# Expert blocks: tokens and weights fetched by SyncE with row numbers in registers, TensorE in a fixed order

## Chip, core and metric

The kernel runs on one core of one Trainium2 chip. The metric is the device time in microseconds. The kernel before took 1066.96 us, the median of three runs (1065.83 to 1073.68).

PE is TensorE (PEld its weight loads), DVE VectorE, ACT ScalarE, POOL GpSimd, SP SyncE. SP computes nothing here; it issues DMAs.

## The reference

One transformer block over 64 sequences of 32 tokens with 256 features (2048 tokens): cross-attention to 257 context rows, self-attention, and a feed-forward layer of 8 experts, of which each token uses the two (`K`) that score highest; an expert has `H` = 512 hidden features. All of it is f32. The change is in the last part:

```python
scores_BSN = jnp.einsum('bsd,nd->bsn', x, Wr) + br
w_BSN = jax.nn.softmax(scores_BSN, axis=-1)
_, idx_BSK = jax.lax.top_k(scores_BSN + biases_N[None, None, :], K)     
val_BSK = jnp.take_along_axis(w_BSN, idx_BSK, axis=-1)
val_BSK = val_BSK / jnp.sum(val_BSK, axis=-1, keepdims=True)
...
h_NM2H = jnp.einsum('md,ndh->nmh', x_MD, Wl1) + bl1[:, None, :]
a_NMH, b_NMH = (h_NM2H[..., :H], h_NM2H[..., H:])
y_NMD = jnp.einsum('nmh,nhd->nmd', jax.nn.silu(a_NMH) * b_NMH, Wl2) + bl2[:, None, :]
ew_MN = ew_MN.at[jnp.arange(M)[:, None], idx_MK].set(val_MK)
y_MD = jnp.einsum('mn,nmd->md', ew_MN, y_NMD)
```

and before it `x = x + xattn(layernorm(x), ctx)`, `x = x + attn(layernorm(x))`; the result is `x + ffn(layernorm(x))`.

## The kernel before

**Start-up.** The attention weights are multiplied into `w_qk` and `w_vo`, and the last context row's contribution is stored in memory as `u_last` (lines 126 to 164). The pool `raw` of these inputs is closed, and later pools take its room.

**Attention.** There are 16 tiles of 128 tokens (four sequences). The main loop (lines 590 to 621) goes through the 64 sequences; each step scores the next sequence (`cross_probs`), transposes the probabilities of this one and mixes its context (`probs_transposed`, `cross_mix`). Two generators run beside it, some steps at a time: `ahead` (the queries of the next two tiles) and `behind`, that is `rest(t)`: cross-attention's output, self-attention and `route(t)` of the tile that was just finished. `load_context` (line 316) fetches the context of the next tile into one of two buffers, and the rows of `u_last` into one of three.

**Routing.** `route` (line 506) normalises the tile into `xr` (256 features, 8 expert weights, the token's number: 265 words), ranks each token within its two experts through a running count `seen`, and scatters `xr` to two rows of `routed` in memory with two indirect DMAs of POOL (line 560). `routed` has 2048 rows for each of the 8 experts. The tile's `x`, with the second bias added, is stored to `out` by SP (line 574). After all tiles `seen` says how many tokens each expert has.

**Experts.** The counts are turned into 39 blocks of up to 128 tokens of one expert each (lines 643 to 688), on DVE, with every row number as a column of 128 words: `sources` (the row of `routed` that each token slot reads; slots beyond the count read one row of zeros, `NOROW`) and `wrows` (the rows of the weight matrix `wall`, with a number out of bounds where the buffer, used three blocks earlier, holds the same expert already). For each block, `gathered` reads 128 rows of `routed` and `weights` reads 128 rows of 12,320 bytes of `wall` (first weights, second weights and first biases of an expert) into one of three buffers `wbuf`; both are indirect DMAs of POOL (lines 704 and 693), and a row out of bounds is skipped. `prepared` transposes the tokens on PE, copies them with ACT (`bxT`), and finds `gate` and the target rows `to` on DVE. `hidden` is 16 products (32 PE instructions, since each f32 product is two) into `pa` and `pb`, four SiLU on ACT (`sa`) and four combinations on DVE (`g`). `combined` is four products of 256 columns (eight instructions) into `py`, a scaling by the gate on DVE (`y`), and an indirect DMA of POOL (line 764) that adds the 128 rows into `out`. Slots beyond the count add into spare rows behind the result.

**What sets the order.** The framework orders each engine's instructions by its own priorities and time estimates, and puts in the waits; no engine's order is written out. The loop at line 778 names block b's work so: gather and weights of b+2, `prepared` and `hidden` of b+1, `combined` of b. POOL's queue has gathers, weights and scatter-adds in one line, and each scatter-add into `out` waits for the one before.

Of the kernel before, what the change touches and what calls it, by code (L numbers as in the profile page):

```python
# [9 lines left out]
FP = mybir.dt.float32  # L10
# [6 lines left out]
P = 128  # L17
D = 256
# [11 lines left out]
NE = 8  # L30
HID = 512
CAP = TOK
NOROW = NE * CAP
RW = D + NE + 1
NBK = (2 * TOK) // P + NE - 1
WLEN = 2 * 2 * HID + 4 * D + 8
WBUF = 3
EPS = 1e-5
BASE = 10000.0
# [7 lines left out]
def block_kernel(  # L47
# [16 lines left out]
    wr_t: bass.AP,  # L64
    br: bass.AP,
    bias_n: bass.AP,
    wall: bass.AP,
    b2: bass.AP,
    out: bass.AP,
):  # L70
    nc = tc.nc

    const = ctx.enter_context(tc.tile_pool(name="const", bufs=1))
    ps = ctx.enter_context(tc.tile_pool(name="ps", bufs=3, space=PSUM))

# [23 lines left out]
    def load(dst, src):  # L99
        nc.sync.dma_start(out=dst, in_=src)  # L100
# [4 lines left out]
    w_qk = const.tile([P, XH, 2, KVD], FP, name="w_qk")  # L105
    w_vo = const.tile([P, XH, D], FP, name="w_vo")

    setup = ExitStack()
    raw = setup.enter_context(tc.tile_pool(name="raw", bufs=1))
    xwq_sb = raw.tile([P, XH // 2, D], FP, name="xwq_sb")  # L110
# [166 lines left out]

    seen = const.tile([P, NE], FP, name="seen")
    nc.gpsimd.memset(seen, 0.0)
    none = const.tile([P, D], FP, name="none")  # L280
    nc.gpsimd.memset(none, 0.0)
    load(routed[NOROW : NOROW + 1, 0:D], none[0:1, :].bitcast(U32))
    load(routed[NOROW : NOROW + 1, D:RW], none[0:1, 0 : RW - D].bitcast(U32))

    load(out[TOK : TOK + P, :], none)

    with ExitStack() as attn:
        kvp = attn.enter_context(tc.tile_pool(name="kv", bufs=2))
# [27 lines left out]
        def load_context(t):  # L316
            kvT = kvp.tile([P, 4, M], FP, tag="kvT", name=f"kvT{t}")
            kvA = kvp.tile([P, 4, MC, KVD], FP, tag="kvA", name=f"kvA{t}")
            ut = u_ring[t % 3]
            load(kvT, ctx_t[:, 4 * t : 4 * t + 4, :])  # L320
            load(kvA, ctx_a[:, 4 * t : 4 * t + 4, :, :])
            for h4 in range(4):
                load(ut[h4 * 32 : h4 * 32 + 16, :], u_last[h4, 16 * t : 16 * t + 16, :])
            return kvT, kvA, ut

        queries = {}

# [178 lines left out]
        def route(t):  # L506
# [52 lines left out]
            for k in range(2):  # L559
                nc.gpsimd.indirect_dma_start(  # L560
                    out=routed[:, :],
                    out_offset=bass.IndirectOffsetOnAxis(ap=slots[:, k : k + 1], axis=0),
                    in_=xr.bitcast(U32),
                    in_offset=None,
                )
            pw = ps.tile([NE, P], FP, tag="t", name=f"pw{t}")
# [19 lines left out]
        kvs = {0: load_context(0)}  # L586
        for _ in cross_queries(0):
            pass
        seqs = [(t, b) for t in range(NT) for b in range(4)]
# [2 lines left out]
        for n, (t, b) in enumerate(seqs):  # L592
            if b == 0:
                cT = wk.tile([P, XH, 4, SEQ], FP, tag="cT", name=f"cT{t}")
                lastT = wk.tile([P, 4, SEQ], FP, tag="lastT", name=f"lastT{t}")
                if t + 1 < NT:
                    kvs[t + 1] = load_context(t + 1)
                if t % 2 == 0 and t + 2 < NT:
                    for j in (t + 2, t + 3):
                        load(xs[j], x[j * P : (j + 1) * P, :])  # L600
                if t % 2 == 1 and t + 1 < NT:
                    ahead = cross_queries((t + 1) // 2)
            if b == 3:
# [12 lines left out]
            next(behind, None)  # L616
            next(ahead, None)
            if b == 3:
                for _ in behind:
                    pass  # L620
                behind = rest(t, cT, lastT, kvs[t][2])
        for _ in behind:
            pass


    with ExitStack() as ffn:
        tb = ffn.enter_context(tc.tile_pool(name="tb", bufs=1))
        xp = ffn.enter_context(tc.tile_pool(name="xp", bufs=3))
# [41 lines left out]
        source = small([NBK], "source")  # L670
        nc.vector.scalar_tensor_tensor(source, ebf, float(CAP), place, ALU.mult, ALU.add)
        nc.vector.scalar_tensor_tensor(
            source, source, float(-NOROW), valid, ALU.add, ALU.mult
        )
        sources = small([NBK], "sources", U32)
        nc.vector.tensor_scalar(sources, source, float(NOROW), None, ALU.add)
# [3 lines left out]
        wrow = small([NBK], "wrow")  # L680
        nc.vector.tensor_scalar(wrow, ebf, float(P), row, ALU.mult, ALU.add)
        held = small([NBK - WBUF], "held")
        nc.vector.tensor_tensor(held, ebf[:, WBUF:], ebf[:, :-WBUF], ALU.is_equal)
# [3 lines left out]
        wrows = small([NBK], "wrows", U32)  # L687
        nc.vector.tensor_copy(wrows, wrow)

        wbuf = [tb.tile([P, WLEN], FP, name=f"wbuf{i}") for i in range(WBUF)]  # L690

        def weights(b):
            nc.gpsimd.indirect_dma_start(  # L693
                out=wbuf[b % WBUF],
                out_offset=None,
                in_=wall[:, :],
                in_offset=bass.IndirectOffsetOnAxis(ap=wrows[:, b : b + 1], axis=0),
                bounds_check=NE * P - 1,
                oob_is_err=False,
            )  # L700

        def gathered(b):
            xg = xp.tile([P, RW], FP, tag="xg", name=f"xg{b}")
            nc.gpsimd.indirect_dma_start(  # L704
                out=xg.bitcast(U32),
                out_offset=None,
                in_=routed[:, :],
                in_offset=bass.IndirectOffsetOnAxis(ap=sources[:, b : b + 1], axis=0),
            )
            return xg  # L710

# [15 lines left out]
        W2, B1 = 4 * HID, 4 * HID + 4 * D  # L727

        def hidden(b, xT):
            w = wbuf[b % WBUF]  # L730
# [21 lines left out]
            return g  # L752

        def combined(b, g, gate, to):
            w = wbuf[b % WBUF]
            py = ps.tile([P, D], FP, tag="a", bufs=2, name=f"py{b}")
            for j in range(4):
                nc.tensor.matmul(  # L758
                    py, g[:, j, :], w[:, W2 + j * D : W2 + (j + 1) * D],
                    start=(j == 0), stop=(j == 3),  # L760
                )
            y = gp.tile([P, D], FP, tag="y", name=f"y{b}")
            nc.vector.tensor_scalar(y, py, gate, None, ALU.mult)  # L763
            nc.gpsimd.indirect_dma_start(  # L764
                out=out[:, :],
                out_offset=bass.IndirectOffsetOnAxis(ap=to[:, 0:1], axis=0),
                in_=y,
                in_offset=None,
                compute_op=ALU.add,
            )  # L770

        xgs = {0: gathered(0)}
        weights(0)
        xgs[1] = gathered(1)
        weights(1)
        ready = {0: prepared(0, xgs.pop(0))}
        gs = {0: hidden(0, ready[0][0])}
        for b in range(NBK):
            if b + 2 < NBK:
                xgs[b + 2] = gathered(b + 2)  # L780
                weights(b + 2)
            if b + 1 < NBK:
                ready[b + 1] = prepared(b + 1, xgs.pop(b + 1))
                gs[b + 1] = hidden(b + 1, ready[b + 1][0])
            _, gate, to = ready.pop(b)
            combined(b, gs.pop(b), gate, to)


# [51 lines left out]
```

## Time and profile before

| | |
|---|---|
| median of 3 runs | 1066.96 us |
| the profiled execution's own time | 1068.11 us |
| its span, first to last instruction | 1066.2 us |
| PE / PEld busy | 933.2 (88%) / 710.0 (67%) |
| DVE / ACT / POOL busy | 586.9 (55%) / 304.2 (29%) / 234.1 (22%) |
| granted PE clock, mean | 0.957 |
| POOL's DMA queue (q0) | 14640 packets, 52.61 MB |
| SP's DMA queue (q1) | 18500 packets, 28.15 MB |
| weight fetch (line 693), from issue to landing, median | 7.1 us |
| gather (line 704) | 4.1 us |
| scatter-add (line 764) | 5.3 us, from 3.7 to 7.8 |
| route scatter (line 560) | 2.7 us, from 2.5 to 5.6 |

Times in the profile count from the first instruction. The cross-attention starts at 51.37 us, the first route scatter is issued at 122.88, the last matmul on `seen` (line 644) runs at 783.66, the first gather is issued at 791.32, the first `pa` starts at 799.81, the first scatter-add at 813.01 and the last at 1059.62. A wait is read as "who waited, then whom for"; the idle time in brackets is that of the engine just before the instruction.

### The profile page before, as it was taken

The page shows a single profiled execution, that of the slowest core. Times are in us where ns is not written, and L with a number is a line of the kernel's source. Part 1 is how long each engine was busy: PE and PEld are TensorE (multiplying, and loading weights), DVE is VectorE, ACT ScalarE, POOL GpSimd, SP SyncE. Part 2 cuts the span into 40 slices and gives each one's busy share as a digit, 9 for nine tenths or more (in the row PEclk, how much of TensorE's full clock was granted, in tenths as well). Part 3 has the DMA queues.
Part 4 walks back from the last instruction along what each step waited for, and adds up shares of the span by engine and source line. Part 5 has one row for each costly group of instructions (what it writes and reads, how often), then busy time and mean ns, then how long its engine had stood idle before and what let it go on. Part 6 is the DMA issues. An engine that isn't in the chain of part 4 may idle for free. (4 is left out here: it accounts for less than half of the span.)

```text
span 1066.2 us, 14917 instructions
## 1 busy us (share of the span) xinstructions
PE 933.2 (88%) x5272; PEld 710.0 (67%) x5272; DVE 586.9 (55%) x2216; ACT 304.2 (29%) x999; POOL 234.1 (22%) x287
## 2 busy tenths in 40 slices
PE   6799989999997998999899899997628988999895
PEld 5567757766774775676577577664418877887785
DVE  3376685765768577566756857666232233332332
ACT  3352332322333232233323323222002222222221
POOL 3100111011011101101101110111033555555562
PEclk9999999998999999899999999998759999999998
DMA  8410101011010110101101010000025666667732
GB/s 259 136 40 4 55 23 38 26 34 54 23 38 26 33 50 28 38 21 38 55 4 55 23 38 26 31 16 13 3 94 206 197 221 178 218 218 219 218 42 25
DMA packets 33215, 81.72 MB, mean 77 GB/s; under 512 B 7435, under 2 KB 23316, under 8 KB 30068
## 3 DMA queue, kind: packets, MB, share of 16 engines
q0 software_dynamic: 14640, 52.61, 16.2%
q1 hardware_dynamic: 18500, 28.15, 8.5%
q8 instruction: 42, 0.69, 0.3%
q14 instruction: 33, 0.27, 0.1%
HBM read 91.66 MB, written 12.73 MB: 98 GB/s over the span
## 5 line engine op out<-in xcount | busy, mean ns | idle before, releaser
L366 ACT ACTIVATE pr<-s,nmx 128x257 f32<-128x257 f32 x256 | 119.8, 473 | 143.2 <-DVE nmx L365 142.4
L361 PE MATMUL s<-kvT,q 128*128 128x257 f32 x512 | 146.8, 413 | 6.8 <-ACT pr L366 6.6
L342 PE MATMUL pq<-xqT,w_qk 128*128 128x256 f32 x512 | 126.0, 388 | 6.2 <-ACT q L83 5.8
L399 PE MATMUL pa<-pt,kvA 128*128 128x512 f32 x256 | 125.6, 613 | 0.3
L361 PEld LDWEIGHTS s<-kvT,q 128*128 128x128 f32 x512 | 94.9, 200 | 39.1 <-ACT pr L366 16.3
L748 DVE SCALAR_TENSOR_TENSOR g<-pb,wbuf,sa 128x128 f32<-128x128 f32 x156 | 43.9, 344 | 127.5 <-PE pb L737 114.9
L409 PE MATMUL po<-w_vo,cT 128*128 128x256 f32 x512 | 113.3, 379 | 0.8 <-DVE cT L402 0.8
L365 DVE TENSOR_REDUCE nmx<-s 128x1 f32<-128x257 f32 x256 | 103.6, 418 | 13.9 <-PE s L361 12.8
L342 PEld LDWEIGHTS pq<-xqT,w_qk 128*128 128x128 f32 x512 | 93.3, 192 | 22.7 <-ACT q L83 8.1
L409 PEld LDWEIGHTS po<-w_vo,cT 128*128 128x128 f32 x512 | 97.0, 191 | 15.5 <-DVE cT L402 2.7
L758 PE MATMUL py<-wbuf,g 128*128 128x256 f32 x312 | 83.5, 392 | 13.2 <-DVE y L763 13.0
L737 PE MATMUL pa<-bxT,wbuf 128*128 128x128 f32 x624 | 80.7, 284 | 15.0 <-DMA wbuf<-in_wall,wrows 14.5
L737 PEld LDWEIGHTS pa<-bxT,wbuf 128*128 128x128 f32 x624 | 77.0, 198 | 23.3 <-issue 21.6
L303 POOL TENSOR_TENSOR rstdr<-ver,minus_half 128x1 f32<-128x1 f32 x16 | 9.3, 584 | 334.6 <-DVE ver L301 334.6
L737 PE MATMUL pb<-bxT,wbuf 128*128 128x128 f32 x624 | 76.4, 276 | 0.0
L391 ACT COPY pt<-tp 128x512 f32<-128x512 f32 x64 | 37.5, 585 | 135.3 <-PE tp L384 135.3
L744 ACT ACTIVATE sa<-pa,wbuf 128x128 f32<-128x128 f32 x156 | 44.5, 368 | 108.7 <-PE pa L737 108.7
L384 PE MATMUL tp<-ident,pr 128*128 128x128 f32 x512 | 74.3, 280 | 0.2
L372 DVE TENSOR_SCALAR pr<-pr,inv 128x256 f32<-128x256 f32 x256 | 73.9, 348 | 0.9
L737 PEld LDWEIGHTS pb<-bxT,wbuf 128*128 128x128 f32 x624 | 73.3, 193 | 0.0
L764 POOL DMA_INDIRECT out_x<-y,to x39 | 62.9, 1613 | 42.7 <-DVE gates L720 24.3
L399 PEld LDWEIGHTS pa<-pt,kvA 128*128 128x128 f32 x256 | 45.3, 193 | 40.1 <-issue 23.4
(194 smaller groups left out, 1194.8 us busy)
## 6 DMA issues: line engine op xcount, KB each, us to landing
kvT<-in_ctx_t SPq DMA_DIRECT2D x16, 514.0 KB, 3.3
kvA<-in_ctx_a SPq DMA_DIRECT2D x16, 512.0 KB, 3.6
x<-in_x SPq DMA_DIRECT2D x16, 128.0 KB, 3.0
out_x<-x SPq DMA_DIRECT2D x16, 128.0 KB, 1.7
xwq_sb<-in_xwq_t SPq DMA_DIRECT2D x1, 1024.0 KB
xwo_sb<-in_xwo SPq DMA_DIRECT2D x1, 1024.0 KB, 9.3
u_last<-u_sb SPq DMA_DIRECT2D x4, 256.0 KB, 3.8
u<-u_last SPq DMA_DIRECT2D x64, 16.0 KB, 1.7
```

The source lines that it names most:

```text
L342: nc.tensor.matmul(pq, w_qk[:, h, k, :], xqT[:, k, :], start=(k == 0), stop=(k == 1))
L361: nc.tensor.matmul(s, qb[:, g * P : (g + 1) * P], kvT[:, b, :], start=True, stop=True)
L365: nc.vector.tensor_reduce(nmx, s, AX.X, ALU.max, negate=True)
L366: nc.scalar.activation(pr[:, g, :], s, AF.Exp, bias=nmx, accum_out=sums[:, g : g + 1])
L372: nc.vector.tensor_scalar(pr[:, g, :ML], pr[:, g, :ML], inv[:, g : g + 1], None, ALU.mult)
L384: nc.tensor.transpose(tp[:, g * P : (g + 1) * P], pr[:, g, j * P : (j + 1) * P], ident)
L399: nc.tensor.matmul(pa, kvA[:, b, j, :], pts[j], start=(j == 0), stop=(j == MC - 1))
L409: nc.tensor.matmul(po, cT[:, h, :, :].rearrange("p b n -> p (b n)"), w_vo[:, h, :], start=(h == 0), stop=False,)
L737: nc.tensor.matmul(dst[:, j, :], w[:, lo : lo + P], xT[:, k, :], start=(k == 0), stop=(k == 1),)
L744: nc.scalar.activation(sa[:, j, :], pa[:, j, :], AF.Silu, bias=w[:, B1 + j : B1 + j + 1])
L758: nc.tensor.matmul(py, g[:, j, :], w[:, W2 + j * D : W2 + (j + 1) * D], start=(j == 0), stop=(j == 3),)
L764: nc.gpsimd.indirect_dma_start(out=out[:, :], out_offset=bass.IndirectOffsetOnAxis(ap=to[:, 0:1], axis=0), in_=y, in_offset=None, compute_ ...
```

## The change

The two fetches of a block leave POOL's queue for SP's. A block's tokens are 128 rows of `routed` one after the other, so one number, the top row, is enough: DVE forms it into `meta[0]`, with the block's expert in `meta[1]` and a flag in `meta[2]` that says whether the weights differ from those fetched three blocks earlier. SP reads these numbers into registers and issues plain DMAs with them; a weight DMA is skipped where the flag is 0. The weight matrix is split into `wall1` (first weights and biases, rows of 8,224 bytes) and `wall2` (second weights, rows of 4,096 bytes), with three buffers each, and both are fetched for block b in iteration b.

As slots beyond the count now read whatever stands in their rows, the whole of `routed` (16,384 rows of 1,060 bytes) is filled with zeros, 2048 rows in each of the first eight steps of the main loop. The row of zeros goes.

SP's order is now the order of the program text, in the whole kernel; PE's is in the expert loop only. There the loop is rewritten in iterations: gather of b+2, `w1` of b, `prepared` of b-1, `hidden` of b-2, `combined` of b-3, `w2` of b. The pool of the gathered tokens has five buffers in place of three. The context of tile 0 is fetched during start-up, its buffers are set up ahead of the pool `raw`, and the rows of `u_last` are fetched in each tile's third step, apart from the context.

```diff
+    SP = mybir.EngineType.SP
+    ctx.enter_context(tc.manual_schedule(engines={SP}))
...
     load(xwo_sb, xwo.rearrange("(c p) k -> p c k", p=P))
+    context0 = load_context(0)
...
-    routed = tc.dram_tile([NOROW + 1, RW], U32, name="routed")
+    routed = tc.dram_tile([NE * CAP, RW], FP, name="routed")
...
+        def load_last(t):
             for h4 in range(4):
-                load(ut[h4 * 32 : h4 * 32 + 16, :], u_last[h4, 16 * t : 16 * t + 16, :])
+                load(
+                    u_ring[t % 3][h4 * 32 : h4 * 32 + 16, :],
+                    u_last[h4, 16 * t : 16 * t + 16, :],
+                )
...
+            if b == 2:
+                load_last(t)
             if b == 3:
                 for _ in ahead:
                     pass
+            if n < NE:
+                load(
+                    routed[n * CAP : (n + 1) * CAP, :].rearrange("(p r) c -> p r c", p=P),
+                    none.to_broadcast([P, CAP // P, RW]),
+                )
...
+        meta = small([3, NBK], "meta", U32)
+        top = small([NBK], "top")
+        nc.vector.tensor_tensor(top, blkf, beginf, ALU.subtract)
+        nc.vector.tensor_scalar(top, top, float(P), None, ALU.mult)
+        nc.vector.scalar_tensor_tensor(top, ebf, float(CAP), top, ALU.mult, ALU.add)
+        nc.vector.tensor_scalar(meta[:, 0, :], top, float(NE * CAP - P), None, ALU.min)
+        nc.vector.tensor_scalar(meta[:, 1, :], ebf, float(NE - 1), None, ALU.min)
+        other = small([NBK], "other")
+        nc.vector.tensor_tensor(other[:, WBUF:], ebf[:, WBUF:], ebf[:, :-WBUF], ALU.not_equal)
+        nc.gpsimd.memset(other[:, :WBUF], 1.0)
         nc.vector.scalar_tensor_tensor(
-            wrow[:, WBUF:], held, float(NE * P), wrow[:, WBUF:], ALU.mult, ALU.add
+            meta[:, 2, :], ebf, float(NE), other, ALU.is_lt, ALU.mult
         )
...
+        def number(k, b, most):
+            return nc.values_load(
+                meta[0:1, k, b : b + 1],
+                engines=[SP],
+                min_val=0,
+                max_val=most,
...
+            )
+
+        def weights(dst, src, b, e, fresh):
+            nc.sync.dma_start(
+                out=dst[b % WBUF],
+                in_=src[bass.ds(e * P, P), :],
+                cond=fresh > 0,
             )
 
         def gathered(b):
             xg = xp.tile([P, RW], FP, tag="xg", name=f"xg{b}")
-            nc.gpsimd.indirect_dma_start(
-                out=xg.bitcast(U32),
-                out_offset=None,
-                in_=routed[:, :],
-                in_offset=bass.IndirectOffsetOnAxis(ap=sources[:, b : b + 1], axis=0),
+            nc.sync.dma_start(
+                out=xg, in_=routed[bass.ds(number(0, b, NE * CAP - P), P), :]
             )
             return xg
...
+        ready, gs, xgs, experts = {}, {}, {}, {}
+        with tc.manual_schedule(engines={mybir.EngineType.PE}):
+            for b in range(-2, NBK + 3):
+                if b + 2 < NBK:
+                    xgs[b + 2] = gathered(b + 2)
+                if 0 <= b < NBK:
+                    experts[b] = number(1, b, NE - 1), number(2, b, 1)
+                    weights(w1buf, wall1, b, *experts[b])
+                if 0 <= b - 1 < NBK:
+                    ready[b - 1] = prepared(b - 1, xgs.pop(b - 1))
+                if 0 <= b - 2 < NBK:
+                    gs[b - 2] = hidden(b - 2, ready[b - 2][0])
+                if 0 <= b - 3 < NBK:
+                    _, gate, to = ready.pop(b - 3)
+                    combined(b - 3, gs.pop(b - 3), gate, to)
+                if 0 <= b < NBK:
+                    weights(w2buf, wall2, b, *experts.pop(b))
```

More of the change, by code (lines that the diff above doesn't have):

```diff
@@ L32 @@
 CAP = TOK
-NOROW = NE * CAP
 RW = D + NE + 1
 NBK = (2 * TOK) // P + NE - 1
-WLEN = 2 * 2 * HID + 4 * D + 8
+W1LEN = 2 * 2 * HID + 8
+W2LEN = 4 * D
 WBUF = 3
@@ L66, in block_kernel @@
     bias_n: bass.AP,
-    wall: bass.AP,
+    wall1: bass.AP,
+    wall2: bass.AP,
     b2: bass.AP,
@@ L106, in block_kernel, with load_context @@
     w_vo = const.tile([P, XH, D], FP, name="w_vo")
+    attn = ExitStack()
+    kvp = attn.enter_context(tc.tile_pool(name="kv", bufs=2))
+    def load_context(t):
+        kvT = kvp.tile([P, 4, M], FP, tag="kvT", name=f"kvT{t}")
+        kvA = kvp.tile([P, 4, MC, KVD], FP, tag="kvA", name=f"kvA{t}")
+        load(kvT, ctx_t[:, 4 * t : 4 * t + 4, :])
+        load(kvA, ctx_a[:, 4 * t : 4 * t + 4, :, :])
+        return kvT, kvA
     setup = ExitStack()
@@ L279, in block_kernel @@
     nc.gpsimd.memset(seen, 0.0)
-    none = const.tile([P, D], FP, name="none")
+    none = const.tile([P, 1, RW], FP, name="none")
     nc.gpsimd.memset(none, 0.0)
[L282 to L288, printed above, removed]
+    load(out[TOK : TOK + P, :], none[:, 0, :D])
+    with attn:
         qp = attn.enter_context(tc.tile_pool(name="q", bufs=3))
@@ L314, in transposed @@
             evacuate(dst, pt)
[L316 to L321, printed above, removed]
+        def load_last(t):
             for h4 in range(4):
-                load(ut[h4 * 32 : h4 * 32 + 16, :], u_last[h4, 16 * t : 16 * t + 16, :])
-            return kvT, kvA, ut
+                load(
+                    u_ring[t % 3][h4 * 32 : h4 * 32 + 16, :],
+                    u_last[h4, 16 * t : 16 * t + 16, :],
+                )
         queries = {}
@@ L562, in route @@
                     out_offset=bass.IndirectOffsetOnAxis(ap=slots[:, k : k + 1], axis=0),
-                    in_=xr.bitcast(U32),
+                    in_=xr,
                     in_offset=None,
@@ L582, in rest @@
             yield from route(t)
-        kvs = {0: load_context(0)}
+        kvs = {0: context0}
         for _ in cross_queries(0):
@@ L620, in block_kernel @@
                     pass
-                behind = rest(t, cT, lastT, kvs[t][2])
+                behind = rest(t, cT, lastT, u_ring[t % 3])
         for _ in behind:
@@ L627, in block_kernel @@
         tb = ffn.enter_context(tc.tile_pool(name="tb", bufs=1))
-        xp = ffn.enter_context(tc.tile_pool(name="xp", bufs=3))
+        xp = ffn.enter_context(tc.tile_pool(name="xp", bufs=5))
         gp = ffn.enter_context(tc.tile_pool(name="gp", bufs=2))
@@ L669, in block_kernel @@
         nc.vector.tensor_tensor(valid, place, manyf, ALU.is_lt)
[L670 to L676, printed above, removed]
         spare = small([NBK], "spare")
         nc.vector.tensor_scalar(spare, valid, 1.0, minus_spare, ALU.subtract, ALU.mult)
-        wrow = small([NBK], "wrow")
@@ L681, in block_kernel @@
-        nc.vector.tensor_scalar(wrow, ebf, float(P), row, ALU.mult, ALU.add)
-        held = small([NBK - WBUF], "held")
-        nc.vector.tensor_tensor(held, ebf[:, WBUF:], ebf[:, :-WBUF], ALU.is_equal)
+        meta = small([3, NBK], "meta", U32)
[3 more added lines that the diff above has]
+        nc.vector.scalar_tensor_tensor(top, ebf, float(CAP), top, ALU.mult, ALU.add)
@@ L686, in block_kernel @@
         )
[L687 to L694, printed above, removed]
-                out_offset=None,
[L696 to L699, printed above, removed]
+        w1buf = [tb.tile([P, W1LEN], FP, name=f"w1buf{i}") for i in range(WBUF)]
@@ new lines, in block_kernel @@
+        w2buf = [tb.tile([P, W2LEN], FP, name=f"w2buf{i}") for i in range(WBUF)]
+        def number(k, b, most):
[4 more added lines that the diff above has]
+                max_val=most,
+                skip_runtime_bounds_check_because="formed from counts that bound it",
+            )
[4 more added lines that the diff above has]
+                cond=fresh > 0,
@@ L703, in gathered @@
             xg = xp.tile([P, RW], FP, tag="xg", name=f"xg{b}")
-            nc.gpsimd.indirect_dma_start(
-                out=xg.bitcast(U32),
-                out_offset=None,
-                in_=routed[:, :],
-                in_offset=bass.IndirectOffsetOnAxis(ap=sources[:, b : b + 1], axis=0),
+            nc.sync.dma_start(
+                out=xg, in_=routed[bass.ds(number(0, b, NE * CAP - P), P), :]
             )
@@ L725, in prepared @@
             return xT, gate, to
-        W2, B1 = 4 * HID, 4 * HID + 4 * D
+        B1 = 4 * HID
         def hidden(b, xT):
-            w = wbuf[b % WBUF]
+            w = w1buf[b % WBUF]
             pa = ps.tile([P, 4, P], FP, tag="s", name=f"pa{b}")
@@ L754, in combined @@
         def combined(b, g, gate, to):
-            w = wbuf[b % WBUF]
+            w = w2buf[b % WBUF]
             py = ps.tile([P, D], FP, tag="a", bufs=2, name=f"py{b}")
@@ L758, in combined @@
                 nc.tensor.matmul(
-                    py, g[:, j, :], w[:, W2 + j * D : W2 + (j + 1) * D],
+                    py, g[:, j, :], w[:, j * D : (j + 1) * D],
                     start=(j == 0), stop=(j == 3),
@@ L770, in combined @@
             )
[L772 to L786, printed above, removed]
+        ready, gs, xgs, experts = {}, {}, {}, {}
[15 more added lines that the diff above has]
+                    weights(w2buf, wall2, b, *experts.pop(b))
 def kernel(**inputs):
@@ L795, with by_row @@
     ctx512 = a["ctx_512"]
+    def by_row(name, n):
+        w = a[f"L0_ffn_{name}"].reshape(NE, n, P, -1)
+        return w.transpose(0, 2, 1, 3).reshape(NE * P, -1)
     laid = {
@@ L814 @@
         "bias_n": a["L0_ffn_biases_N"],
-        "wall": np.concatenate(
-            [
-                w.reshape(NE, n, P, -1).transpose(0, 2, 1, 3).reshape(NE * P, -1)
-                for w, n in ((a["L0_ffn_Wl1"], 2), (a["L0_ffn_Wl2"], 4), (a["L0_ffn_bl1"], 8))
-            ],
-            axis=1,
-        ),
+        "wall1": np.concatenate([by_row("Wl1", 2), by_row("bl1", 8)], axis=1),
+        "wall2": by_row("Wl2", 4),
         "b2": a["L0_ffn_bl2"],
```

## The prediction

> **What bounds the kernel now.** I read the table of stretches first, because the share of busy time is a mean over an attention part that the change hardly touches and an expert part that it rewrites. Columns: stretch and its length, then busy us (and instructions) of PE, PEld, DVE, ACT, POOL, then granted PE clock, DMA share, GB/s.
>
> ```profile
> 50.00:760.00 710.00, 649.85 (x3374) 466.36 (x3372) 474.64 (x1773) 226.62 (x759) 78.20 (x119) 0.97 0.10 31
> 760.00:800.00 40.00, 15.32 (x74) 8.79 (x75) 15.72 (x73) 2.03 (x5) 9.57 (x10) 0.54 0.18 64
> 800.00:1020.00 220.00, 198.52 (x1394) 176.74 (x1395) 67.43 (x266) 51.09 (x166) 114.50 (x97) 0.98 0.65 204
> 1020.00:1055.00 35.00, 33.20 (x241) 30.47 (x240) 11.13 (x42) 8.70 (x29) 16.07 (x13) 1.00 0.27 35
> ```
>
> Attention runs to about 785 us with PE 92% busy and the DMA engines nearly idle. From 800 the experts run: PE is busy 90% with DMA at 0.65, and 95% in the last stretch, where no weights are fetched. The waits of PE in the experts come next (total us, times, longest):
>
> ```profile
> PE pa L737 <- DMA wbuf<-in_wall,wrows: 14.5, 15, 5.0
> PE py L758 <- DVE y L763: 13.0, 36, 0.4
> ```
>
> So PE stands for late weights, and once per block for the eviction `y`. The timeline of a block without weight fetches says what a block costs (start, us, then the group):
>
> ```profile
> 1018.44 1.95 PE L737 MATMUL pa<-bxT,wbuf 128*128 128x128 f32 x16
> 1020.23 1.95 PE L737 MATMUL pb<-bxT,wbuf 128*128 128x128 f32 x16
> 1022.01 1.46 PE L758 MATMUL py<-wbuf,g 128*128 128x256 f32 x6
> 1023.31 0.38 PE L716 MATMUL pxT<-ident,xg 128*128 128x128 f32 x2
> 1024.05 0.70 PE L758 MATMUL py<-wbuf,g 128*128 128x256 f32 x2 [0.36 <-DVE y L763]
> 1024.59 0.27 PE L737 MATMUL pa<-bxT,wbuf 128*128 128x128 f32 x1
> ```
>
> From `pa` to `pa` a block is 1024.59 - 1018.44 = 6.15 us. By starts, 32 matmuls of `pa` and `pb` take 3.57; six of `py` take 1.30, so eight 1.73; two transposes take 0.22. That is 5.52 of work; the other 0.63 is the `y` wait (0.36) and the refill behind it. Last I read POOL's timeline, in a stretch with weights and at the end:
>
> ```profile
> 906.68 1.01 POOL L693 DMA_INDIRECT wbuf<-in_wall,wrows  x1 [1.92 <-ACT bxT L718]
> 908.00 1.62 POOL L764 DMA_INDIRECT out_x<-y,to  x1 [0.30 <-issue]
> 909.92 0.99 POOL L704 DMA_INDIRECT xg<-routed,sources  x1 [0.31 <-issue]
> 912.83 1.00 POOL L693 DMA_INDIRECT wbuf<-in_wall,wrows  x1 [1.92 <-ACT bxT L718]
> 915.32 1.62 POOL L764 DMA_INDIRECT out_x<-y,to  x1 [1.49 <-DVE gates L720]
> ...
> 1055.00 1.56 POOL L764 DMA_INDIRECT out_x<-y,to  x1 [4.57 <-DVE y L763]
> 1059.62 1.56 POOL L764 DMA_INDIRECT out_x<-y,to  x1 [3.05 <-DMA out_x<-y,to]
> ```
>
> The last line is the key: each scatter-add into `out` waits until the one before has landed. The 39 of them are a serial chain: 4.62 us a link when nothing else moves (3.86 to land, 0.76 to start), but 7.32 at 908.00, behind 1.58 MB of weights that POOL queued 1.3 us earlier. I put the 915.32 start down to that chain, although the row names `gates`: the landing, seen from a DVE wait at 914.55, is 0.77 before it, as at the end. From the first scatter-add (813.01) to the last (1059.62) the mean of 38 links is 6.49 us. Both serial things, PE and chain, run above their own floors because of the weights.
>
> **The change, part by part.** Of POOL's 52.6 MB on its queue, 32 route scatters and 39 gathers of 0.136 MB and 39 scatter-adds of 0.131 MB leave 37.9 MB, which is 24 weight fetches of 1.577 MB: 24 blocks of 39 load (three per expert), before and after alike. No byte of weights is saved.
>
> *Weights and gathers to SP.* POOL loses 39 x (1.01 + 0.30) and 39 x (0.98 + 0.30) = 101 us of queue time, none of it on the path by itself; what counts is order. Now `wbuf` of block b+2 can only be asked for when block b-1's `py` is done, about one 6.2 us block before use, and lands 7.1 after the request. After: `w1` of block b waits for `hidden(b-3)`, `w2` for `combined(b-3)`, and PE's order puts two whole blocks and a transpose between that and use. The longest string: `combined(b-3)` ends; SP issues `w2(b)`, reads a row number, issues a gather, reads two numbers, issues `w1(b+1)`. An SP issue is 0.43 us in the rows. A register load has no row: from below it is an SP semaphore event (0.02), from above POOL's indirect issue with its gap (1.28); I take the SP issue, 0.45, the nearest kind. So 3 x 0.43 + 3 x 0.45 = 2.6 to issue; landing of 1.05 MB between `kvT` (514 KB, 3.3) and `wbuf` (1.58 MB, 7.1) is 5.2; `w2` and the gather ahead in the ring add about 1.7. Sum 9.5, against 2 x 5.52 + 0.22 = 11.3 until `hidden(b+1)`. With 1.28 a load it is 12.0, and a loading block 0.35 late. Most likely covered: the 14.5 us of weight waits go, and PE and chain are next.
>
> The Trainium skill speaks against this part: its page "DMA: Bandwidth & Descriptors", section "Rules for kernel authors", says that spreading DMAs over SP, ACT and GpSimd doesn't help bandwidth, since all run on the same 16 engines, and saves only issue time. By it alone the gain would be nil. The rows differ in what they price: POOL's queue was late by order, not by bandwidth (DMA share 0.65). The page's section "Latency and other measured facts" gives a floor of about 0.6 us for a register load from memory, which no run here shows; by that the string would be 9.9.
>
> *PE in fixed order.* Per iteration: transposes of b-1, `hidden` of b-2, `combined` of b-3. Each reads what was evicted an iteration (5.5 us) earlier: `bxT` 0.37, `sa` 1.14, `g` 1.12, `y` 0.48, so the 0.36 wait and its refill lose their cause. What waits is then in line: a late `xg` holds `hidden` and `combined` behind it, but gathers are three iterations ahead. `y`, with two buffers, ties PE to the chain: late scatter-adds stop it two blocks later. PE floor: 5.52.
>
> *The chain.* POOL holds nothing but scatter-adds, and weights go by another queue, so a scatter-add no longer stands behind all of a 12 KB-row fetch; it still shares engines with it. How much that costs is the unknown. From below 0 (4.62 a link), from above the old queueing, 2.7 (7.32). The nearest rows: a route scatter lands in 2.7 us at the median, and in 4.8, 3.0, 4.0 and 3.9 where SP's 512 KB `kvA` with 4 KB rows moves beside it, +1.2 on the mean. `w1` rows are twice as long, so +2.4, `w2` rows +1.2; weighted by bytes 2.0; the weights are moving in some 0.8 of a loading block (5.7 of 7.1 us). So 2.0 x 0.8 = 1.6, a link of 6.2 in loading blocks. In the other 15 blocks it lies between 4.62 (catching up) and PE's 5.52; the middle is 5.07. Mean (24 x 6.2 + 15 x 5.07)/39 = 5.77.
>
> *Start of the experts.* Seven small DVE operations go, seven come. SP then reads five numbers and issues three gathers before `w1(0)`: 790.9 + 5 x 0.45 + 3 x 0.43 = 794.4, landed at 799.6; now `pa` starts at 799.81. Zero (-2 to +4 by the bounds of a load). First scatter-add and the 6.6 us after the last start stay.
>
> *Zero fills.* Eight of 2.17 MB, issued by SP: four when the start-up loads are out (about 36 us), four behind `kvA` of tile 2 (74.5 now). 1 KB rows to memory ran at 220 to 310 GB/s in the profile's `u_last` stores, so four take 28 to 40 us: done by 76 and 115. The first route scatter, which must wait for them, is at 122.9. `u` of tile 0, behind two fills, lands near 60; it is read at 82. Zero, covered by those 8 to 20 us.
>
> *SP in program order, first context early.* SP's waits (out stores, `kvA`) now hold later loads, but each context is needed some 45 us after its buffer is free. `kvT` is on the chip earlier, yet at 51.37 `s` followed `pq` without a wait. Zero; the rest of the schedule may fall otherwise, +-5.
>
> **Sum.** 38 x (6.49 - 5.77) = 27.4. The profiled execution took 1068.1 us (span 1066.2), 1.1 above the median of 1066.96: span to 1038.8, median to 1040.
>
> **Rivals.**
> (A) The chain stays as slow as now because SP's rows crowd it as POOL's did. For it: 7.32 at 908. Against it: +1.2 beside `kvA`. Link 7.32 in loading blocks: mean (24 x 7.32 + 15 x 5.07)/39 = 6.45, gain 1.5, 1065.
> (B) SP's serial string becomes the bound. Loads of 1.28 us give a loading block of 5.9 and leave the chain the bound, near 1040 to 1045. It ends slower by 1% only from a mean of 6.77, that is 7.55 in loading blocks, a string of 15.3 and a load of 2.4 us; 1078 there. Against it: no control row on SP is that long.
> (C) Slower: the fills are late, the route scatter of tile 0 stands on POOL, and behind it the `rstd` and `xb` that PE needs. Decides when the fills end later than 122.9 + 11 (POOL's idle time there) + 38, i.e. below about 128 GB/s; at 110 they end at 194: 60 lost, 1100. Against it: the 220 to 310 of `u_last`.
> (D) The chain hides better than I think and PE alone bounds: 5.52 a block, gain 36.9, 1030.
>
> **How the numbers follow.** Forecast 0.62 (links of 5.52 to 6.07: 1030 to 1051), A 0.14 (1052 to 1067), B 0.07, C 0.09, faster than 1030 0.05, other losses 0.03. About 1% (10.7 us) is what a measurement can tell from no change. Faster: 0.62 + 0.05 + 0.05 of A + 0.02 of B = 0.74; within 1%: 0.09 of A, 0.02 of B, 0.03 of C = 0.14; slower: 0.03 of B, 0.06 of C, 0.03 = 0.12. The range reaches from PE's floor less 3 of schedule to the end of A: 1027 to 1066.
>
> **What would show it.** Right: no PE wait on `w1buf` after the third block; no `py` wait on `y` in the non-loading blocks; `pa` to `pa` near 5.5 there; scatter-add starts 6.2 apart in loading blocks; tile 0's route scatter at its old time. Wrong: PE waiting for weights in each loading block (B), scatter-adds over 7 apart (A), POOL standing at 123 (C), or attention of another length.

## The result and the profile after

The changed kernel took 1102.0 us (median of four runs, 1097.6 to 1103.25) beside 1068.1 for the kernel before (four runs): a ratio of 1.0302, 95% interval 1.0252 to 1.0352. It is slower; the forecast was 1040, faster. The profiled execution took 1101.59 us with a span of 1099.7.

Instructions that both kernels have split the span into five stages (us): the matmul `po<-u,lastT` of tile 0 and of the last tile, the first and the last scatter-add.

| stage | before | after | difference |
|---|---|---|---|
| start to `po` of tile 0 | 82.27 | 88.71 | +6.4 |
| on to `po` of the last tile | 673.63 | 683.14 | +9.5 |
| on to the first scatter-add | 57.11 | 58.27 | +1.2 |
| first to last scatter-add | 246.61 | 261.36 | +14.8 |
| after the last | 6.58 | 8.22 | +1.6 |
| span | 1066.2 | 1099.7 | +33.5 |

The expert loop, which was to gain 27.4, lost 14.8. The table of stretches of the changed kernel, in the columns of the one above, has it in these two lines:

```profile
816.00:1050.00 234.00, 197.97 (x1369) 183.29 (x1369) 55.31 (x256) 50.85 (x165) 46.65 (x30) 0.94 0.63 193
1050.00:1087.00 37.00, 37.00 (x265) 34.56 (x266) 11.68 (x46) 8.71 (x29) 10.97 (x8) 1.00 0.26 33
```

While weights move, PE is busy 85% (it was 90%); at the end 100%. So PE's order is good and something holds it under load. Of the waits of all engines in that part, four lines (total, times, longest):

```profile
POOL out_x L781 <- DVE gates L737: 185.9, 33, 7.8
DVE to L741 <- DMA out_x<-y,to: 184.8, 34, 8.2
...
PE py L775 <- DVE y L780: 35.3, 18, 3.5
...
PE pa L754 <- DMA w1buf<-in_wall: 5.2, 1, 5.2
```

The last line is good news: PE waited for weights once, at the first block (14.5 us in 15 waits before). The `y` wait, which was to go, grew from 13.0 to 35.3. The first two are the loss: DVE stood 185 us at a one-column operation, `to`, waiting for a scatter-add to land, and POOL, which issues the next scatter-add, waited as long for DVE. `to` has five buffers; `to` of block b+5 may be written only when the scatter-add of block b, which reads the old contents, has landed. DVE's order, laid out by the framework, has behind it the four `g` of block b+2 and the `y` of block b+1. The timeline of one turn, all engines, cut to this chain:

```profile
943.50 1.55 POOL L781 DMA_INDIRECT out_x<-y,to  x1 [6.17 <-DVE gates L737]
...
950.73 0.16 DVE L741 TENSOR_TENSOR to<-xg,spare 128x1 uint32<-128x1 f32 x1 [7.43 <-DMA out_x<-y,to]
...
950.88 1.12 DVE L765 SCALAR_TENSOR_TENSOR g<-pb,w1buf,sa 128x128 f32<-128x128 f32 x4
951.91 0.47 DVE L780 TENSOR_SCALAR y<-py,gate 128x256 f32<-128x256 f32 x1
...
952.44 1.65 PE L775 MATMUL py<-w2buf,g 128*128 128x256 f32 x3 [3.37 <-DVE y L780]
952.66 1.55 POOL L781 DMA_INDIRECT out_x<-y,to  x1 [7.61 <-DVE gates L737]
```

The scatter-add of 943.50 lands before 950.73; only then do `to`, `g` and `y` run, and the next scatter-add starts 1.93 us behind the start of `to`. The chain of scatter-adds now runs through DVE's queue: in 34 of the 38 links the next one starts 1.95 to 1.96 us behind the landing, in the last four 0.75. The name that POOL's row gives (`gates`) is the last small operation that DVE finished, not the cause. Where `to` no longer has a successor, the detour ends; POOL's own timeline shows the step:

```profile
1061.64 1.55 POOL L781 DMA_INDIRECT out_x<-y,to  x1 [4.22 <-DVE gates L737]
1067.36 1.55 POOL L781 DMA_INDIRECT out_x<-y,to  x1 [4.17 <-DVE gates L737]
1073.14 1.55 POOL L781 DMA_INDIRECT out_x<-y,to  x1 [4.22 <-DVE y L780]
1077.78 1.55 POOL L781 DMA_INDIRECT out_x<-y,to  x1 [3.08 <-DMA out_x<-y,to]
```

5.72 and 5.78 a link become 4.64, with no weights moving in either. Over the loop the mean link is 261.36 / 38 = 6.88 (6.49 before).

Of the 9.5 us of attention 9.0 fall between the `po` of tile 1 (131.30 before, 137.74 after) and that of tile 2 (172.69, 188.08), where tile 0 is routed. POOL's timeline there:

```profile
141.30 1.22 POOL L567 DMA_INDIRECT routed<-xr,rslots  x1 [23.32 <-DMA u<-u_last]
...
146.87 0.58 POOL L313 TENSOR_TENSOR rstds<-ves,minus_half 128x1 f32<-128x1 f32 x1
```

The first route scatter, due near 129 (122.88 and the 6.4 of the start), went at 141.30; the `rstds` that PE's next transposes need stood behind it. The row names the loads of `u`, which share their semaphores with the zero fills; the trace has the last fill landing at 137.88 and POOL past its waits for the fills at 137.90. The 3.4 us from there to the start are not explained.

### The profile page after: what moved, and what is told of

Same layout as the page of the kernel before. It is cut to its first block, busy times and chain, and to the rows that moved or that the text cites. A ratio compares the mean times of both kernels' runs of the same rounds, so it can differ in the third digit from the quotient of the medians.

```text
span 1099.7 us, 15304 instructions
## 1 busy us (share of the span) xinstructions
PE 940.5 (86%) x5272; PEld 723.5 (66%) x5272; DVE 576.5 (52%) x2216; ACT 304.3 (28%) x999; POOL 154.0 (14%) x210
## 3 DMA queue, kind: packets, MB, share of 16 engines
q0 software_dynamic: 7152, 9.46, 4.7%
## 5 line engine op out<-in xcount | busy, mean ns | idle before, releaser
L368 PEld LDWEIGHTS s<-kvT,q 128*128 128x128 f32 x512 | 95.3, 201 | 38.6 <-ACT pr L373 15.6
L349 PEld LDWEIGHTS pq<-xqT,w_qk 128*128 128x128 f32 x512 | 93.8, 193 | 29.6 <-ACT q L86 14.8
L775 PE MATMUL py<-w2buf,g 128*128 128x256 f32 x312 | 82.3, 410 | 35.4 <-DVE y L780 35.3
L741 DVE TENSOR_TENSOR to<-xg,spare 128x1 uint32<-128x1 f32 x39 | 6.2, 159 | 184.8 <-DMA out_x<-y,to 184.8
L781 POOL DMA_INDIRECT out_x<-y,to x39 | 60.6, 1554 | 227.7 <-DVE gates L737 185.9
L775 PEld LDWEIGHTS py<-w2buf,g 128*128 128x128 f32 x312 | 59.1, 199 | 47.9 <-DVE y L780 40.3
L754 PE MATMUL pa<-bxT,w1buf 128*128 128x128 f32 x624 | 81.3, 287 | 5.2 <-DMA w1buf<-in_wall 5.2
L754 PEld LDWEIGHTS pa<-bxT,w1buf 128*128 128x128 f32 x624 | 78.4, 204 | 5.6 <-issue 5.6
L754 PE MATMUL pb<-bxT,w1buf 128*128 128x128 f32 x624 | 77.2, 277 | 0.0
L754 PEld LDWEIGHTS pb<-bxT,w1buf 128*128 128x128 f32 x624 | 74.0, 195 | 0.0
L391 PEld LDWEIGHTS tp<-ident,pr 128*128 128x128 f32 x512 | 62.6, 146 | 9.1 <-issue 3.1
(193 smaller groups left out, 1099.7 us busy)
```

What stands on the lines that cost most here:

```text
L349: nc.tensor.matmul(pq, w_qk[:, h, k, :], xqT[:, k, :], start=(k == 0), stop=(k == 1))
L368: nc.tensor.matmul(s, qb[:, g * P : (g + 1) * P], kvT[:, b, :], start=True, stop=True)
L391: nc.tensor.transpose(tp[:, g * P : (g + 1) * P], pr[:, g, j * P : (j + 1) * P], ident)
L754: nc.tensor.matmul(dst[:, j, :], w[:, lo : lo + P], xT[:, k, :], start=(k == 0), stop=(k == 1),)
L775: nc.tensor.matmul(py, g[:, j, :], w[:, j * D : (j + 1) * D], start=(j == 0), stop=(j == 3),)
L781: nc.gpsimd.indirect_dma_start(out=out[:, :], out_offset=bass.IndirectOffsetOnAxis(ap=to[:, 0:1], axis=0), in_=y, in_offset=None, compute_ ...
```

## The experiments

Three causes were to be told apart first: VectorE's wait, the fills, the order of start-up.

**Own `to` buffers.** In the changed kernel:

```diff
-            to = xp.tile([P, 1], U32, tag="to", name=f"to{b}")
+            to = tb.tile([P, 1], U32, name=f"to{b}")
```

> Every block's row numbers `to` get a buffer of their own, so VectorE no longer waits for the scatter-add five blocks back before it makes the next `g` and `y`. Theory (VectorE's queue is part of the chain: landing 3.8 to 7.4, then to 0.27, g 1.03, y 0.39, start 0.67): the 34 waits of `to` (184.8 us in all) go, a link shortens by about 1.2 us, to landing plus 0.76 or PE's 5.5 a block, whichever is longer; first to last scatter-add falls from 261.4 to some 215 to 235 us, the time by 26 to 45 us, to 1057 to 1076. Rival (the weights on SP's queue slow each landing, and the scatter-adds only queue elsewhere): waits move from VectorE to POOL, the stretch stays at 255 to 262, the time falls by less than 7 us. The first 800 us stay as they are in both.

Measured: 1046.74 us, ratio to before 0.9796 (0.9754 to 0.9837). Every engine's order stayed the same; only the wait went. First to last scatter-add fell to 218.77, and PE ran at its floor, as its timeline shows (starts 5.52 apart):

```profile
820.08 1.95 PE L754 MATMUL pa<-bxT,w1buf 128*128 128x128 f32 x16
825.60 1.95 PE L754 MATMUL pa<-bxT,w1buf 128*128 128x128 f32 x16
```

The waits of the same kernel show what is left, VectorE's `y` on the scatter-add two blocks back, of which 7.2 us reach PE:

```profile
DVE y L780 <- DMA out_x<-y,to: 71.4, 22, 6.1
...
PE py L775 <- DVE y L780: 7.2, 7, 2.4
```

So the theory holds: every link but one is now the landing plus 0.75, and 34 links of 1.2 us less are the 41 of the 42.6 us that the loop lost. The time is lower than expected because the first 800 us did not stay as they were (821.4 us to the first scatter-add in place of 830.1), which the repeat below takes up.

**Long fill rows.** Each partition's 16 rows written as one of 16,960 bytes:

```diff
-    none = const.tile([P, 1, RW], FP, name="none")
+    none = const.tile([P, CAP // P, RW], FP, name="none")
...
-                    routed[n * CAP : (n + 1) * CAP, :].rearrange("(p r) c -> p r c", p=P),
-                    none.to_broadcast([P, CAP // P, RW]),
+                    routed[n * CAP : (n + 1) * CAP, :].rearrange("(p r) c -> p (r c)", p=P),
+                    none.rearrange("p r c -> p (r c)"),
```

> The eight zero fills are written as 128 rows of 16,960 bytes each in place of 2048 rows of 1,060 bytes, from a zero tile of the same size; bytes and places in SP's order are the same. Theory (the 1,060-byte rows at 200 to 220 GB/s keep the DMA engines full until 141 us and hold the first route scatter and POOL behind it): fills end by 115 or earlier, the first route scatter is back near its old distance from attention's start, the wait of `trs` on `xns` (6.4) goes, the time falls by 9 us, to about 1093. Rival (the route scatter is held by something else, or long rows are no faster): no change, 1102, first route scatter still near 141.

**Loads first.** The four `u_last` stores, and the close of the pool `raw` with them, moved behind the nine loads from `base` to `b2_sb`:

```diff
-    for h4 in range(4):
-        r = h4 % 2 * NB
...
-    setup.close()
-
...
     load(b2_sb, b2)
+    for h4 in range(4):
+        r = h4 % 2 * NB
...
+    setup.close()
```

> The nine loads of rope base, self-attention and router weights stand ahead of the four u_last stores in SP's program order; all else is the same. Theory (SP stands from 9.5 to 28.5 for u_sb, and the rope table on ScalarE for `base` behind it, which costs PE 12.6 us of waits at 31 to 44): `po` of tile 0 starts at 82 to 84 in place of 88.7, the time falls by 6.4 us, to about 1095. Rival (the delay comes from the fills or from ScalarE's new order): `po` of tile 0 stays near 88, the time within 2 us of 1102.

**All three.**

> The three edits together: own `to` buffers, long fill rows, loads ahead of the u_last stores. Theory (the three causes are separate places and add up): falls of 35, 9 and 6.4 us, 1052 (1041 to 1061), faster than the kernel before by 7 to 25 us. Rival (they overlap, or the landing under weights is the whole of the last part): 1080 to 1090, no faster than before.

Measured: long rows 1085.77 us (ratio 1.0166, 1.0132 to 1.02), loads first 1089.84 (1.0193, 1.014 to 1.0246), all three 1046.59 (0.9771, 0.971 to 0.9831). Both single edits seem to gain beside 1102, and together they add nothing to own `to` buffers. With long rows the first route scatter went at 128.73, 40.6 behind the `po` of tile 0 as before the change; with loads first that `po` came at 87.10, not at 82 to 84. This called for the changed kernel itself once more.

> The changed kernel as it is, once more, beside the others on one chip. Question: whether the late first route scatter (141.3 us in its profile) belongs to the kernel or to that execution, since the version with own `to` buffers, the same up to 785 us, had it at 129.56. Theory (the fills end within a few us of the scatter, so a few per cent of DMA rate decide): first scatter between 128 and 142, time 1088 to 1103. Rival (the stall belongs to the kernel, and the other versions lost it by their edits): 141 and 1102 again.

Measured: 1084.81 us (1081.57 to 1087.42), ratio 1.0138 (1.0083 to 1.0192); first route scatter at 130.50. The kernel is slower than before here too, but by 1.4%, not 3.0%. The DMA engines moved 227 GB/s from 50 to 58 us, where the first profile had 205, full in both, and the loop took 256.4 in place of 261.4. So the first profile's stall is real but sits at an edge: here the last fill landed at 127.21, just ahead of the scatter, where the first profile had 137.88. Some 10% of DMA rate decide. It seems to have gone with the session and not with the single execution, since all four times of the first session (1097.6 to 1103.25) lie above all four of this one; what made it differ, no run tells. The 17 us between the two medians are only in part the stall: of 14.0 us of span, 6.5 lie in attention and 4.9 in the loop. By the ratios, which take each session's own kernel before, long rows and loads first gained nothing over this repeat (1.0166 and 1.0193 beside 1.0138), and own `to` buffers gained 38 us (37 by the two ratios), all of it in the loop (256.42 to 218.77).

Why loads first gained nothing, two rows of its timelines of ACT and PE show:

```profile
34.06 1.28 ACT L221 ACT_TABLE_LOAD   x1 [5.67 <-DMA u_last<-u_sb]
```

```profile
41.49 14.87 PE L349 MATMUL pq<-xqT,w_qk 128*128 128x256 f32 x56 [11.05 <-ACT q L86]
```

`base` was fetched early (issued at 9.46), yet its use still began at 34: the rope tiles and `q` lie where the pool `raw` lay, and `raw` is free only when the `u_last` stores, its last readers, have landed. That held before the change too. What differs is VectorE's and ScalarE's order: before, `q` copies ran from 34.03 on, between the steps of the rope chain; now the whole chain (two table loads, a 2.9 us power on POOL) goes first, and `q` begins at 40.8.

**Own memory for the start.** Own `to` buffers, loads first, fill rows of 4,240 bytes, and:

```diff
-    u_sb = raw.tile([P, XH // 2, D], FP, name="u_sb")
+    u_sb = const.tile([P, XH // 2, D], FP, name="u_sb")
...
-    with tc.tile_pool(name="rope", bufs=1) as rp:
+    with ExitStack():
+        rp = const
```

> Own `to` buffers, loads ahead of the u_last stores, fill rows of 4,240 bytes (all as in the version with three edits, whose rows are 16,960), and new: the rope tiles and u_sb lie in memory of their own instead of the set-up pool's, which later tiles take over. Theory (the start was late because rope set-up and the first `q` copies wait at 34 for the u_last stores to land, only to free that memory, and the whole rope chain now stands ahead of `q`): PE's 11.0 us wait of `pq` on `q` goes, `po` of tile 0 starts at 76 to 81 in place of 88.6, the time falls by 7 to 11 us from 1046.6, to about 1038. Rival (the start is held by the loads themselves, or the gain is given back at the first route scatter): 1044 or more.

Measured: 1035.91 us (ratio 0.9692, 0.9623 to 0.9761), and 1035.39 (0.9704, 0.9651 to 0.9758) when run again:

> The version with own `to` buffers, loads first, fill rows of 4,240 bytes and own memory for the rope set-up, once more, as the base of the three beside it: 1033 to 1042, first route scatter near 120.3 without a wait on the fills.

`po` of tile 0 came at 79.69 and 77.63, and by the ratios (0.9771 for all three edits) the gain is some 8 us; PE's long wait is gone:

```profile
36.02 12.87 PE L350 MATMUL pq<-xqT,w_qk 128*128 128x256 f32 x56 [0.46 <-ACT xqT L86]
```

This version is faster than both kernels, and is the base of the runs with short rows, five `y` buffers and three weight fetches.

**Short fill rows on that base.** The fills back to rows of 1,060 bytes.

> The same base with the fills in their first form, rows of 1,060 bytes, so that tile 0's route scatter, ready at about 120, meets fills that ended at 124 to 141 in the profiles with such rows. Theory (a late fill holds POOL, and the next tile's rstd behind it, and so PE): the scatter starts when the fills end, 124 or later, and what is over POOL's slack of a few us shows in the time: 2 to 14 us longer than the base. Rival (the scatter has slack enough, the 9.0 us seen in the first profile had another cause): scatter late but time within 2 us of the base.

Measured: 1053.35 us, 18.0 more than its base. POOL and PE:

```profile
142.01 1.22 POOL L568 DMA_INDIRECT routed<-xr,rslots  x1 [32.16 <-DMA u<-u_last]
...
147.92 0.57 POOL L314 TENSOR_TENSOR rstds<-ves,minus_half 128x1 f32<-128x1 f32 x1
```

```profile
149.00 0.69 PE L324 MATMUL trs<-ident,xns 128*128 128x128 f32 x2 [15.59 <-DVE xns L317]
```

The last fill landed at 140.87. Counted from the `po` of tile 0, the scatter is 20.8 us later than in the base (142.01 - 80.58 in place of 118.24 - 77.63) and PE stands 15.6: POOL's slack is about 5 us. The changed kernel's first profile gives the same: 12.0 later than before the change, and a `trs` wait of 6.4. So late fills do cost what that profile showed, and what makes them late is the row length, the only difference to the base: 209 GB/s here against 387 with 4,240 bytes (in the same 50 to 58 us, engines full in both).

**The kernel before with own `to` buffers.** The same one-line edit there.

> The kernel before, with a buffer of its own for every block's `to`, nothing else. Theory (there the scatter-adds were slow because they stood behind weights in one queue, and VectorE's wait for `to`, 32.3 us in 21 waits of up to 3.0, was mostly slack): 1060 to 1068. Rival (VectorE's wait was already part of the chain before the change, so that removing it is worth as much there as after): 1030 to 1050, and the change of queues itself is worth little.

Measured: 1068.16 us, ratio 0.9988 (0.9961 to 1.0015). VectorE's 32.3 us of waits for `to` went and the time did not move: in the old order that wait was slack. The changed kernel, with its new queues and order, has it in the chain.

**TensorE's order left to the framework**, with own `to` buffers:

```diff
-        with tc.manual_schedule(engines={mybir.EngineType.PE}):
+        with ExitStack():
```

> Own `to` buffers, and TensorE's expert part ordered by the framework instead of by hand; it puts `py` of a block right behind `pa` and `pb` of the same block. Theory (the fixed order is needed: `py` waits for the last `sa` and `g` of its own block, some 1.5 to 2 us behind `pb`): a block of 7 to 7.5 us, PE waits of 55 to 75 us on `g`, time 1100 to 1125. Rival (the chain of scatter-adds bounds at 5.8 whatever PE does): within 10 us of 1047.

Measured: 1063.21 us, 16.5 more than with the fixed order; the loop took 236.4. The theory's direction holds, but it had put the loss at 53 to 78 us. PE's timeline says why it is less:

```profile
901.22 1.95 PE L754 MATMUL pb<-bxT,w1buf 128*128 128x128 f32 x16
903.66 2.00 PE L775 MATMUL py<-w2buf,g 128*128 128x256 f32 x8 [0.50 <-DVE g L765]
```

`py` waits 0.50 for its own block's `g`, and a block takes 6.28 (907.50 - 901.22), not 7 to 7.5.

**Five `y` buffers** on the base with own memory.

> The same base with five buffers for `y` in place of two. Theory (what is left over PE's 5.52 a block is `y` waiting for the scatter-add two blocks back: 65.7 us of VectorE's waits, of which 7.6 reach PE): PE's waits of `py` on `y` go, time 6 to 9 us shorter than the base, near 1028. Rival (the chain itself is as long as PE's work, so that the waits move to the last scatter-add): within 3 us of the base.

Measured: 1041.67 us (1038.38 to 1042.3; the base 1034.8 to 1044.13): no gain. PE's waits on `y` are gone, and POOL's wait for the last scatter-add grew (31.0 and 39.2 us in the two profiles of the base):

```profile
POOL out_x L784 <- DMA out_x<-y,to: 89.5, 22, 8.6
```

The loop took 219.92, as before (219.23 and 216.63): PE started its last `pa` at 1009.47, and the chain drained until 1032.15. The rival holds: the chain alone needs 5.79 a link, since every link but one is the landing plus 0.75.

**Three weight fetches only**, on the same base.

```diff
-        nc.vector.tensor_tensor(other[:, WBUF:], ebf[:, WBUF:], ebf[:, :-WBUF], ALU.not_equal)
+        nc.vector.memset(other[:, WBUF:], 0.0)
```

> The same base, but weights are fetched for the first three blocks only; every later block computes with those, so 21 of 24 fetches are left out. Theory (weights moving beside a scatter-add slow its landing, from 3.8 to 5 to 8 us): the long links of 6 to 8 us vanish, every link is 4.4 to 5.6, and the loop is PE's 5.52 a block; first to last scatter-add falls from 219 to about 210, the time by 8 to 10 us. Rival (long links come from VectorE or PE, not from the weights): links of 6 to 8 stay, time within 3 us.

It leaves out the weights that later experts need, and serves the time alone. Measured: 1028.07 us, 7.3 less than its base; the loop took 207.97. POOL:

```profile
904.51 1.55 POOL L784 DMA_INDIRECT out_x<-y,to  x1 [3.97 <-DVE gate L742]
910.03 1.55 POOL L784 DMA_INDIRECT out_x<-y,to  x1 [3.96 <-DVE gate L742]
```

All links but the first three and the last two are 5.52, PE's pace, with POOL idle for work. The scatter-adds landed in 3.7 to 5.1 us, median 3.8, where the base's took 3.7 to 8.7, median 4.2. So weights beside a scatter-add do slow it, and that costs 9 to 11 us of the loop in the base.

| stage (us) | changed, again | own `to` | own `to`, free order | + own memory | + short rows | + 5 `y` | + 3 fetches |
|---|---|---|---|---|---|---|---|
| to `po` of tile 0 | 87.99 | 87.10 | 87.85 | 79.69 | 80.58 | 79.47 | 80.42 |
| to the last `po` | 676.68 | 675.92 | 673.80 | 673.71 | 694.37 | 676.64 | 674.33 |
| to the first scatter-add | 56.33 | 58.38 | 55.17 | 56.21 | 56.66 | 56.12 | 56.48 |
| to the last | 256.42 | 218.77 | 236.38 | 219.23 | 215.64 | 219.92 | 207.97 |
| rest | 8.28 | 8.23 | 8.20 | 8.26 | 8.25 | 8.25 | 8.20 |

The column "+ own memory" is the first of its two profiles; the second has 77.63, 674.34, 56.18, 216.64 and 8.2.

## Why the prediction was wrong, point by point

**The step that failed: the chain.** Forecast and measured time lie 62 us apart, and 42 of these are in the loop, where 246.6 - 27.4 = 219.2 was forecast and 261.4 measured. "POOL holds nothing but scatter-adds" counted a link as landing plus 0.76. It looked at the queue that issues the scatter-add and not at the queue that feeds it. The waits of before had the row, and VectorE's timeline of before what stands around it:

```profile
DVE to L724 <- DMA out_x<-y,to: 32.3, 21, 3.0
```

```profile
912.08 0.48 DVE L763 TENSOR_SCALAR y<-py,gate 128x256 f32<-128x256 f32 x1
...
914.55 0.16 DVE L724 TENSOR_TENSOR to<-xg,spare 128x1 uint32<-128x1 f32 x1 [1.79 <-DMA out_x<-y,to]
...
919.11 0.48 DVE L763 TENSOR_SCALAR y<-py,gate 128x256 f32<-128x256 f32 x1
```

I used the wait to read landings (914.55) and did not ask what stands behind `to` on VectorE. Before, the next scatter-add (915.32) had its `y` at 912.08, ahead of the waiting `to`; the `y` behind it (919.11) was for the scatter-add after that. In the changed kernel the `y` of the very next scatter-add stands behind the waiting `to`. So no wait was added by the change; an old one came to stand in the chain. A link became landing plus 1.96, and because PE's turn hangs on the same `g` and `y`, PE could not get ahead. One line that gives `to` memory of its own undoes it, worth 38 us.

**The size of the chain otherwise: right in the mean, by luck.** 5.77 was forecast; with the detour gone it is 5.757, 5.769 and 5.70, and 5.787 where PE is out of its way. But it is not 24 links of 6.2 and 15 of 5.07: with own `to` buffers 18 links are over 5.3 us, with a mean of 7.01, and 20 below it, with a mean of 4.63. A link with weights beside it is some 2.4 longer and not 1.6, and there are fewer of these: two errors that cancel. Nor did the gain come from where it was expected. From issue to landing the first 38 scatter-adds took 5.09 us on the mean before, 5.05 in the changed kernel and 5.00 with own `to`: taking the weights out of POOL's queue did not make the landing shorter on the mean. What fell is the time from a landing to the next start, 1.40 on the mean before (18 of 38 over 0.9) and 0.76 with own `to`; 38 x (1.40 - 0.76) is 24 of the 27.8 us between 246.61 and 218.77. In the last stretch before, without weights, these links are 6.14 long, PE's block.

**Weights and gathers on SP: right.** No wait for weights after the first block. The string runs as costed: with own `to`, from `w2` to the gather 0.86, from there to `w1` 1.38; less 0.33 and 0.34 of the issue before, a row number is 0.53, and 0.52 each for the two (taken: 0.45). Of that the register load itself is 0.27, the median of 117 on SP. The floor of about 0.6 in the Trainium skill ("DMA: Bandwidth & Descriptors", section "Latency and other measured facts") is above these rows, which decide. The rule of that page that was weighed, that spreading DMAs over issuing engines brings no bandwidth, is not contradicted: the gain is in order, and a link is still some 2.4 us longer when weights pass.

**PE in fixed order: right.** With it `pa` to `pa` is 5.52 wherever PE does not wait, and the fixed order is worth 16.5 us against the framework's on the same queues. That `y` with two buffers ties PE to the chain is true and costs nothing, since the chain ends last.

**Start of the experts: right within 1.2 us.** The 1.6 us more behind the last scatter-add are in every version with SP's written order; no run here tells what they are.

**SP in program order: zero taken, 3 to 6 us lost.** The `po` of tile 0 came at 82.27 before, and at 84.58 in the version of before with own `to`, whose first 800 us are the same; in the changed kernel at 88.71 and 87.99. The loss is not in a late load, as I first thought, but in the order that the framework then chose on VectorE and ScalarE around a wait for memory; which part of the change made it choose so, no run separates. The +-5 was about the right bound for it.

**Zero fills: zero taken, up to 9.5 us lost.** The rate was read from the `u_last` stores (220 to 310); with the fills, `u` rows and contexts together the DMA engines moved 198 to 235 from 40 to 130 us, the first four fills began at 41 and the second four at 81 (36 and 74.5 were taken), and the 8 to 20 us of cover were gone. In the repeat the same stage lost 3.0. The rival C had the mechanism. It allowed POOL 11 us of slack, and there are about 5. Its edge at 128 GB/s is no edge of the stall: the 38 us in it come to the forecast gain of 27.4 and 10.7 more, so it marks where the fills alone would turn the gain into a clear loss. Here they were one loss of several.

**The other rivals.** A (the chain as slow as now, 1065) named the right place with the wrong cause; it had a mean link of 6.45, and VectorE made it 6.88. B (SP's string) and D (PE alone) did not decide; the loop of D, 5.52 a link, is what the run with three fetches shows. All of them assumed that the work on VectorE was free to run, and the range left C out.

## What to carry to other kernels

A buffer's release is a wait like any other: when stages are spread over more iterations, list for each engine which instruction frees a reused tile, by whose completion, and what stands behind it in that engine's order; a tile of four bytes per partition never deserves a wait. When work goes to another queue, look for the serial chain in all queues that feed the link, not only in the one that issues it. And a large background transfer is not hidden by the average: find the first instruction that must wait for its end, and what its engine does next.

## What the runs showed of the hardware

Rows of 1,060 bytes written to memory kept all 16 DMA engines full at 205 to 231 GB/s from 50 to 58 us, in six profiles; the same bytes in rows of 4,240 went at 387 and 403, and of 16,960 at 425 and 432. The Trainium skill ("DMA: Bandwidth & Descriptors", section "Specifications") puts the shortest transfer for full rate at 512 bytes; here a row of twice that length got about half the rate. While PE stood for the late route scatter, the clock granted to it fell, and the stop cost more than the 15.6 us of that wait: the stage is 20.0 longer than the base's (694.37 and 674.34). The table of stretches of the version with short rows (columns as above):

```profile
138.00:146.00 8.00, 0.00 (x0) 0.00 (x0) 0.00 (x0) 0.00 (x0) 1.65 (x2) 0.50 0.27 94
...
150.00:154.00 4.00, 4.00 (x9) 2.46 (x8) 1.96 (x6) 1.70 (x6) 0.00 (x0) 0.57 0.00 0
```

PE had been at work again since 149.00; its granted clock was still 0.57 from 150 to 154, and 1.00 in the four us after. By an estimate from such rows (0.50 of the 1 us up to 150, 0.43 of the 4 behind it) that is some 2 of the 4.4 us; the rest is not accounted for.
